# Two layers on one core: the norm of image 0 gets its own place in the order, and places and shares are settled anew

## The chip, the cores and the metric

The kernel runs on one core of a Trainium2 chip, in one launch. The core has TensorE (PE) for matmuls and transposes, VectorE (DVE), ScalarE (ACT) and GpSimd (POOL) for work on elements, and a sequencer (SP) that issues nearly all DMAs. The metric is the device time in microseconds (us); lower is better.

## The reference: a selective scan, then an attention block between convolutions

The input `x` has 4 images of 512 channels and 32 x 32 points (1024 tokens), all float32.

```
# layer 0, xn = LayerNorm over channels of GroupNorm(x)
xm, z = split(xn @ W_in)                    # 1024 channels each
xs = silu(causal depthwise conv of 4 taps (xm))
dt, B, C = parts of xs @ W_x;  dt = softplus(dt @ W_dt + b_dt)
h[t] = exp(dt[t]*A) * h[t-1] + (dt[t]*xs[t]) * B[t]     # 16 states per channel
y = sum over states of h*C + xs*D;  x = x + (y * silu(z)) @ W_out
# layer 1, on GroupNorm(x)
top, center = two 1x1 convolutions;  bottom = 3x3 convolution
x = x + conv3x3(v + softmax(center @ top) @ bottom),  v = GroupNorm(x)
```

Layer 1 can't begin on image 0 before the GroupNorm statistics of image 0's layer-0 output are there. They need only image 0, while layer 0 ends with image 3.

## The kernel before

**Stages and units.** Layer 0 treats the images one after the other. An image has 8 stages `n` (4 groups of 256 channels, `e`, by 2 halves of 512 tokens, `h`; `n = 2e + h`), and a stage has 16 units, one for each state `s`. A unit (`unit`, from L886) makes a decay with ACT exponentials (L904), a product with B, a scan on DVE (L957), a product with C, and a sum over states by accumulating transposes on PE into `y` (L990). Who makes the two products differs:

- **ACT unit**: ACT makes the product with B, transposed (four `sc` instructions, L917), PE turns it back (eight transposes into `u`, L943), DVE scans, POOL makes the product with C (L980).
- **POOL unit**: POOL makes the product with B (L932, from the row `bbc` that a DMA spreads over the partitions), DVE scans, POOL makes the product with C (L980).
- **DVE unit**: as the POOL unit, but the scan goes to PSUM and DVE makes the product with C (two of L973). In a first half, DVE copies two carries as well (L962), where POOL would copy them (L979).

The table `ACT_B[b][n]` holds the number of ACT units of a stage, and `DVE_C[b][n]` says how many of the rest are DVE units.

**The order.** Nothing of layer 0 is issued as written: each piece is a `step` with an engine, a guessed duration and a place `prio`. Unit `s` of stage `n` of image `b` has the place `(8b + n)*16 + s`, so that the images begin at 0, 128, 256 and 384 and the last unit has 511. `Plan.issue` (L149) walks through a clock of its own. On each engine it takes, among the steps that could start within `SLACK` of the soonest, the one with the lowest place. No step may be issued whose place is more than `AHEAD` beyond the lowest one still open (pieces marked `fill` don't count as open, but are held by it too). A step that needs another ACT table is held back by `TURN` times 1.3 us, unless its place is over `URGENT` lower than the best that needs none. On the chip each engine runs its instructions in the order so found.

**What else has places.** All of them are in `PRM`. For the next image: the norm (`m0`, spread by `nl`), projection with convolution (`c0`, `cg`), the parameters of the scan (`p0`, `pg`). For the present one: the gates (`g0`, `gg`), the step sizes (`dl`; `d1`, `d2` for image 0), the transposes of a unit against its other parts (`kt`, `ke`, `ka`). Then the output projection of the image before (`o0`, `og`), of the last image in parts as its stages end (`l3`, `l5`, `l6`; `last_proj`, L1103), and 18 pieces of a weight transform for layer 1 (`pc`; `transform`, L1224) that mostly run on POOL, in the tile `work`.

**The norm of image 0** (`first_image`, L1148) ends layer 0. POOL clears the rim of the padded tile (L281 to L284), in the memory that `work` had, so after the last transform piece. SP reads image 0 back in eight DMAs (L1166), DVE makes statistics (L1179, L1180), PE averages groups (L1187, L1203), ACT takes the root (L304, L305), DVE normalizes (L1217). With `fi=-5.11` and `fl=0` the loads have the place 517.11, the statistics up to the root 521.11 (`prio + 4`), the normalizing 522.11. The last gate (DVE, L1030 and L1033) has 514, the last output projection (PE, L444, into `po`) 512, 514, 516 and 518 for its four blocks, and so have the additions of `po` to `total` (DVE, L1134).

After that each engine goes on with layer 1 in the order written: PE with the scores (`pt`, L1411; `psc`, L1432) and the 3 x 3 convolutions (`m_b`, `m_o`, L1584).

Of the kernel before, what the change touches and what calls it, by code (L numbers as in the profile page):

```python
# [29 lines left out]

PRM = dict(
    xp=(1, 2, 1),
    d1=10.1,
    pg=(0.46, 0.4, 0.67, 0.61),
    kt=(0.33, 3.93, 5.81, 6.9),
    ke=(1.1, 4.93, 2.75, 4.55),
    ka=(-4.81, -1.6, -3.24, 3.25),
    dl=(9.79, 12.5, 12.12, 15.22),
    nl=(0.17, 1.94, 1.25),
    m0=(52.74, 50.42, 48.4),  # L40
    c0=(68.39, 60.05, 64.33),
    cg=(4.46, 6.19, 6.58),
    p0=(117.51, 108.54, 112.88),
    g0=(1.18, -46.47, -50.81, -55.84),
    gg=(7.81, 8.86, 8.96, 7.61),
    o0=(17.38, 16.29, 17.48),
    og=(5.73, 4.85, 7.27),
    pc=(-196.09, -39.49, -79.97, -11.49, -76.67, -112.89, -101.52, 31.36, 14.53, 57.53, 92.72, 155.74, 200.22, 264.5, 322.22, 362.01, 463.04, 499.85),
    h0=-6.05,
    hg=2.38,  # L50
    p1=3.61,
    d2=-7.19,
    fl=0,
    fi=-5.11,
    l3=69.43,
    l5=101.89,
    l6=114.08,
    il=0,
)


ACT_B = (
# [4 lines left out]
)  # L67
DVE_C = (
# [4 lines left out]
)  # L73


# [22 lines left out]
class Plan:  # L98
# [4 lines left out]
    LAG = {"PE": 0.17, "DVE": 0.095, "ACT": 0.1, "POOL": 0.06, "SP": 0.0}  # L103
    HOP = {"PE": 0.16, "DVE": 0.045, "ACT": 0.06, "POOL": 0.08, "SP": 0.05}
    BEGIN = {"PE": 5.0, "DVE": 1.5, "ACT": 9.0, "POOL": 7.0, "SP": 1.5}
    FREE, LOAD, SLACK, AHEAD = 0.06, 1.3, 0.11, 15.44
    TURN, URGENT = 1.47, 1.72

    def __init__(self, slots, in_order, exp_set):
        self.slots, self.steps, self.exp_set = dict(slots), [], exp_set  # L110
# [5 lines left out]
    def step(self, eng, us, fn, reads=(), writes=(), prio=0.0, table=None, kb=0, fill=False, holds=()):  # L116
        s = Step(eng, us, fn, prio, table, kb, fill)
        for b in holds:
            if b.first:
                s.deps.add(b.first)  # L120
            else:
                b.first = s
        for b in (*reads, *writes, *holds):
            if b in s.bufs:
                continue
            s.bufs.append(b)
            if b.ring and not b.left:
                s.takes.append(b)
                if b.ring in self.queues and not b.free:
                    self.queues[b.ring].append(b)  # L130
            b.left += 1
        for b in reads:
            if b.writer:
                s.deps.add(b.writer)
        for b in writes:
            s.deps.update(b.readers)
            if b.writer:
                s.deps.add(b.writer)
        for b in reads:
            b.readers.append(s)  # L140
        for b in writes:
            b.writer, b.readers = s, []
        s.deps.discard(s)
        for d in s.deps:
            d.users.append(s)
        s.unmet = len(s.deps)
        self.steps.append(s)
# [69 lines left out]
def mamba_then_pab_kernel(  # L217
# [60 lines left out]
    def padded(b, pool, tag):  # L278

        xg = pool.tile([P, NCC, HH + 2, WW + 2], F32, tag=tag, name=f"xg_{b}")  # L280
        nc.gpsimd.memset(xg[:, :, 0, :], 0.0)  # L281
        nc.gpsimd.memset(xg[:, :, HH + 1, :], 0.0)
        nc.gpsimd.memset(xg[:, :, 1 : HH + 1, 0], 0.0)
        nc.gpsimd.memset(xg[:, :, 1 : HH + 1, WW + 1], 0.0)  # L284
        return xg
# [16 lines left out]
    def rsqrt(out, var):  # L302

        nc.scalar.activation(out, var, AF.Ln, bias=eps)  # L304
        nc.scalar.activation(out, out, AF.Exp, scale=-0.5)  # L305

    def deviation(p, mv, mean, dev):


        nc.vector.tensor_copy(mean, p[:, :NCC])  # L310
        nc.vector.tensor_sub(dev, mv[:, :, 0], p[:, :NCC])
        nc.vector.tensor_sub(p[:, NCC : 2 * NCC], mv[:, :, 0], p[:, :NCC])
        nc.vector.tensor_mul(p[:, 2 * NCC : 3 * NCC], dev, p[:, NCC : 2 * NCC])
        nc.vector.tensor_add(dev, p[:, 2 * NCC : 3 * NCC], mv[:, :, 1])
# [8 lines left out]
    with ExitStack() as l0:  # L323
# [76 lines left out]
        step = plan.step  # L400
# [3 lines left out]
        def buf(ring, shape, name, free=False):  # L404
            if ring is None:
                return Buf(None, lambda: shape)
            if ring in cells:
                y, x = shape[1:3]
                return Buf(
                    ring,  # L410
                    lambda: cells[ring].pop(0).rearrange("p (y x o) -> p y x o", y=y, x=x),
                    done=lambda t: cells[ring].append(t.rearrange("p y x o -> p (y x o)")),
                )
            pool = {"xt": xtp, "mm": mmp, "u": up, "y0": yp, "y1": yp}.get(ring, sp)
            return Buf(
                ring,
                lambda: pool.tile(shape, F32, tag=ring, name=name, bufs=plan.slots[ring]),
                free=free,
            )
# [728 lines left out]
        def first_image(prio):  # L1148

            spl = {}  # L1150
            stat = buf(None, None, "")
            chunks = [buf(None, None, "") for c in range(NCC)]

            def inner(c):
                return image[0][:, c, 1 : HH + 1, 1 : WW + 1]

            def make():
                image[0] = padded(0, cpool, "image")

            step("POOL", 1.2, make, [], [pieces, *chunks], prio - PRM["fl"])  # L1160
            for c in range(NCC):
                for h in range(NH):
                    n = HH // NH
                    step(
                        "SP", 0.4,
                        lambda c=c, h=h, n=n: nc.sync.dma_start(  # L1166
                            inner(c)[:, h * n : (h + 1) * n, :],
                            x1[0][h][c * P : (c + 1) * P, :].rearrange("p (h w) -> p h w", w=WW),
                        ),
                        [x1s[0][h]], [chunks[c]], prio - PRM["fl"], kb=768,  # L1170
                    )

                def stats(c=c):
                    if c == 0:
                        spl["mv"] = spool.tile([P, NCC, 2], F32, tag="mv", name="mv_image")
                    bs = spool.tile([P, NH, 6], F32, tag="bs", name=f"bs_image_{c}")
                    n = HH // NH
                    for h in range(NH):
                        nc.vector.bn_stats(bs[:, h, :], inner(c)[:, h * n : (h + 1) * n, :])  # L1179
                    nc.vector.bn_aggr(spl["mv"][:, c, :], bs)  # L1180

                step("DVE", 1.45, stats, [chunks[c]], [stat], prio + 4)
            prio += 4
            pm = buf("mm", [P, T], "pm_image")
            step(
                "PE", 0.3,
                lambda: nc.tensor.matmul(  # L1187
                    pm()[:, :NCC], gm_sb, spl["mv"][:, :, 0], start=True, stop=True
                ),
                [stat], [pm], prio,  # L1190
            )

            def mid():
                spl["mean"], spl["dev"] = (
                    spool.tile([P, NCC], F32, tag=n, name=f"{n}_image") for n in ("gmean", "gdev")
                )
                deviation(pm(), spl["mv"], spl["mean"], spl["dev"])

            step("DVE", 0.75, mid, [], [pm, stat], prio)
            pv = buf("mm", [P, T], "pv_image")  # L1200
            step(
                "PE", 0.3,
                lambda: nc.tensor.matmul(  # L1203
                    pv()[:, :NCC], gm_sb, spl["dev"], start=True, stop=True
                ),
                [stat], [pv], prio,
            )

            def root():
                spl["rstd"] = spool.tile([P, NCC], F32, tag="grstd", name="grstd_image")  # L1210
                rsqrt(spl["rstd"], pv()[:, :NCC])

            step("ACT", 1.7, root, [pv], [stat], prio, "exp")
            for c in range(NCC):
                step(
                    "DVE", 0.76,
                    lambda c=c: nc.vector.tensor_scalar(  # L1217
                        inner(c), inner(c), spl["mean"][:, c : c + 1],
                        spl["rstd"][:, c : c + 1], ALU.subtract, ALU.mult,
                    ),  # L1220
                    [stat], [chunks[c]], prio + 1,
                )
# [628 lines left out]
```

## Time and profile before

| | us |
|---|---|
| median of 3 runs | 2886.27 (2882.78 to 2889.2) |
| the profiled execution | 2896.7 |
| its span, first to last instruction | 2894.9 |
| start of the last copy out of `y`, which ends image 0, 1, 2, 3 | 585.9, 1026.2, 1490.3, 1860.1 |
| first matmul of layer 1 on PE (`pt`) | 1875.8 |

In the views below, each stretch lists the busy time of each engine with the number of its instructions, then the granted clock of PE (1.00 is full) and the DMA share. A group line gives its busy time, the mean duration in nanoseconds, and the idle time just before its instructions with what ended it. A timeline line gives start, duration, engine, line, operation and tiles.

### The profile page before, as it was taken

How to read it: one execution, taken by the hardware profiler on the slowest of the kernel's cores; microseconds unless marked ns; L12 is line 12 of the kernel's file. 1: busy time of each engine (PE TensorE's matmuls, PEld its weight loads, DVE VectorE, ACT ScalarE, POOL GpSimd, SP SyncE). 2: the span in 40 equal slices, each digit the busy share in tenths (PEclk: the TensorE clock that was granted, in tenths of full speed). 3: DMA queues.
4: the chain of work that ended last, by engine and by line, in shares of the span. 5: the costliest groups of instructions: out<-in, count | busy, mean ns of one | idle time of the engine just before them, and what ended most of it. 6: DMA issues, size and time to landing. Idle time of an engine off the chain costs nothing.

```text
span 2894.9 us, 36258 instructions
## 1 busy us (share of the span) xinstructions
PE 2720.9 (94%) x11752; PEld 1628.6 (56%) x11752; DVE 2288.4 (79%) x2730; ACT 1837.1 (63%) x3250; POOL 2039.3 (70%) x1243
## 2 busy tenths in 40 slices
PE   6898799999999999989989999899999999999999
PEld 2466566666666666666667766544444444444445
DVE  4579999989999889989899999867776755346264
ACT  4789999999899999899999999530300003030000
POOL 6999999899998999999999999733241341214222
PEclk9999999999999999999999999899999999999999
DMA  6766655567655577645565664757789886536586
GB/s 182 209 178 190 190 166 176 159 216 243 197 163 167 161 230 229 200 144 179 160 203 178 210 196 147 180 215 259 257 277 304 315 322 240 188 123 240 189 318 241
DMA packets 406548, 603.68 MB, mean 209 GB/s; under 512 B 47224, under 2 KB 246136, under 8 KB 382040
## 3 DMA queue, kind: packets, MB, share of 16 engines
q1 hardware_dynamic: 398744, 587.11, 63.6%
q10 hardware_dynamic: 7616, 14.26, 1.3%
q8 instruction: 94, 1.54, 0.2%
q14 instruction: 94, 0.77, 0.1%
HBM read 504.27 MB, written 96.99 MB: 208 GB/s over the span
## 4 chain that ended last, share of the span: by engine, by line
PE 44%; ACT 19%; DVE 15%; POOL 9%; issue 6%; DMA 5%; SPq 0%; POOLq 0%; DVEq 0%; ACTq 0%
PE m_o L1584 10%; PE m_b L1584 8%; DVE da L957 5%; ACT sc L917 4%; PE y L990 4%; PE pat L1643 4%; ACT da L904 4%; PE u L943 3%; POOL da L980 3%; PE pxm L444 3%; PE po L444 3%; ACT u L904 3%; PE pz L444 2%; DVE u L957 2%; PE pp L800 1%
## 5 line engine op out<-in xcount | busy, mean ns | idle before, releaser
L980 POOL TENSOR_TENSOR da<-da,cbc 128x1024 f32<-128x1024 f32 x314 | 741.6, 2368 | 33.3 <-DVE da L957 8.3
L917 ACT ACTIVATE sc<-dtxt,bt_sb 128x256 f32<-128x256 f32 x1256 | 550.7, 499 | 17.1 <-PE u L943 16.4
L932 POOL TENSOR_TENSOR dbx<-dtx,bbc 128x1024 f32<-128x1024 f32 x198 | 467.1, 2369 | 20.2 <-PE y L990 7.8
L904 ACT ACTIVATE da<-dt,a_sb 128x512 f32<-128x512 f32 x628 | 433.7, 714 | 15.4 <-PE y L990 10.6
L957 DVE TENSOR_TENSOR_SCAN da<-da,u 128x512 f32<-128x512 f32 x328 | 383.1, 1203 | 40.5 <-PE u L943 23.3
L943 PE MATMUL u<-ident,sc 128*128 128x128 f32 x2512 | 363.1, 279 | 33.4 <-DVE da L957 19.6
L943 PEld LDWEIGHTS u<-ident,sc 128*128 128x128 f32 x2512 | 291.6, 142 | 161.6 <-issue 47.2
L957 DVE TENSOR_TENSOR_SCAN da<-da,carry_sb,u 128x512 f32<-128x512 f32 x300 | 367.2, 1260 | 13.7 <-PE u L943 10.3
L990 PE MATMUL y<-ident,da 128*128 128x128 f32 x2512 | 339.5, 277 | 27.7 <-POOL da L980 27.0
L1584 PE MATMUL m_b<-uw_b,v_b 128*128 128x512 f32 x768 | 335.2, 596 | 6.7 <-DMA uw_b<-u_b 4.4
L990 PEld LDWEIGHTS y<-ident,da 128*128 128x128 f32 x2512 | 290.3, 142 | 90.2 <-POOL da L980 49.0
L1584 PE MATMUL m_o<-uw_o,v_o 128*128 128x512 f32 x736 | 321.9, 596 | 4.2 <-DMA uw_o<-u_o 4.1
L904 ACT ACTIVATE u<-dt,a_sb 128x512 f32<-128x512 f32 x396 | 262.5, 681 | 10.7 <-DVE da L957 5.8
L444 PE MATMUL pxm<-xt,winc 128*128 128x345 f32 (+3 forms) x704 | 242.7, 488 | 18.6 <-DVE xs L706 4.7
L1584 PEld LDWEIGHTS m_b<-uw_b,v_b 128*128 128x128 f32 x768 | 145.5, 191 | 192.9 <-issue 178.6
L444 PE MATMUL pz<-xt,winc 128*128 128x512 f32 x512 | 240.3, 600 | 2.1 <-ACT dtxt L881 1.0
L1584 PEld LDWEIGHTS m_o<-uw_o,v_o 128*128 128x128 f32 x736 | 139.0, 191 | 180.2 <-issue 173.2
L990 PE MATMUL y<-ident,dbx 128*128 128x128 f32 x1584 | 219.8, 276 | 12.2 <-DVE dbx L973 7.1
L980 POOL TENSOR_TENSOR dbx<-dbx,cbc 128x1024 f32<-128x1024 f32 x91 | 215.2, 2365 | 13.8 <-DVE dbx L957 7.0
L1643 PE MATMUL pat<-y_b,st 128*128 128x512 f32 x512 | 221.6, 593 | 1.7 <-DVE rz L1654 1.6
L990 PEld LDWEIGHTS y<-ident,dbx 128*128 128x128 f32 x1584 | 182.6, 142 | 48.4 <-issue 22.1
L444 PE MATMUL po<-gt,wpr 128*128 128x512 f32 x384 | 182.4, 594 | 4.3 <-DVE u L957 2.3
(231 smaller groups left out, 4113.2 us busy)
## 6 DMA issues: line engine op xcount, KB each, us to landing
cbc<-bcd SPq DMA_DIRECT2D x512, 256.0 KB, 3.6
uw_b<-u_b SPq DMA_DIRECT2D x96, 1024.0 KB, 4.8
uw_o<-u_o SPq DMA_DIRECT2D x92, 1024.0 KB, 4.8
bbc<-bcd SPq DMA_DIRECT2D x198, 256.0 KB, 4.1
u_b<-work SPq DMA_DIRECT2D x192, 128.0 KB, 2.7
winc<-in_w_in_dram SPq DMA_DIRECT2D x72, 256.0 KB, 3.6
szd<-sz SPq DMA_DIRECT2D x32, 512.0 KB, 3.7
szl<-szd SPq DMA_DIRECT2D x32, 512.0 KB, 5.0
```

What stands on the lines that cost most here:

```text
L444: lambda k=k, lhs=lhs, rhs=rhs: nc.tensor.matmul(p()[:, at : at + cols], lhs(), rhs(), start=(k == 0), stop=(k == n - 1)),
L800: lambda d=d, hs=hs, pp=pp: nc.tensor.matmul(pp()[p0 : p0 + NP, :], wx_sb[:, d, :], xs[b, d]()[:, hs], start=(d == 0), stop=(d == NDC - 1),),
L904: nc.scalar.activation(t, dt()[:, j], AF.Exp, scale=a_sb[:, at : at + 1])
L917: nc.scalar.activation(sc()[:, k], dtxt()[:, k], AF.Copy, scale=bt[:, at, s : s + 1])
L932: lambda: nc.gpsimd.tensor_mul(hc(), dtx(), b_bc().to_broadcast([P, 2, T])),
L943: nc.tensor.transpose(u()[:, k * P : (k + 1) * P], sc()[:, k, j, :], ident)
L957: nc.vector.tensor_tensor_scan(ht, *((hc()[:, j], u()) if on_act else (u(), hc()[:, j])), carry_sb[:, j, s : s + 1] if h else 0.0, ALU.mul ...
L980: nc.gpsimd.tensor_mul(hc(), hc(), c_bc().to_broadcast([P, 2, T]))
L990: nc.tensor.matmul(y[j]()[:, k, :], hc()[:, j, k * P : (k + 1) * P], ident, start=(s == 0 and k == 0), stop=(s == NS - 1 and k == NK - 1), ...
L1584: nc.tensor.matmul(m[q], v[:, q, k, c, :], w[:, c, :], start=(c == 0), stop=(c == NCC - 1 and not extra),)
L1643: nc.tensor.matmul(pt, st[m][:, 2 * P * j + h : 2 * P * (j + 1) : 2], xb[m // 2][:, m % 2, :], start=(m == 0), stop=(m == NMC - 1),)
```

## The change

One parameter is new, `f4`: the statistics of image 0's norm have the place `fi`-based `prio + f4` in place of `prio + 4`, and all that follows them in the norm moves with them. Their guessed duration goes from 1.45 to 1.4. With the new `fi`, `fl` and `f4` the loads stand at 517.36, the statistics up to the root at 512.29, the normalizing at 513.29. Most other entries of `PRM` change too, seven entries of the two tables of shares, and `AHEAD`, `TURN` and `URGENT`. No instruction of a kind that was not there is added. Lines from `f4` on stand one line lower.

```diff
-    d1=10.1,
-    pg=(0.46, 0.4, 0.67, 0.61),
-    kt=(0.33, 3.93, 5.81, 6.9),
-    ke=(1.1, 4.93, 2.75, 4.55),
-    ka=(-4.81, -1.6, -3.24, 3.25),
-    dl=(9.79, 12.5, 12.12, 15.22),
-    nl=(0.17, 1.94, 1.25),
-    m0=(52.74, 50.42, 48.4),
-    c0=(68.39, 60.05, 64.33),
-    cg=(4.46, 6.19, 6.58),
-    p0=(117.51, 108.54, 112.88),
-    g0=(1.18, -46.47, -50.81, -55.84),
-    gg=(7.81, 8.86, 8.96, 7.61),
+    d1=6.86,
+    pg=(0.58, 0.48, 0.67, 0.62),
+    kt=(0.48, 3.9, 6.11, 5.12),
+    ke=(0.94, 4.77, 3.54, 3.15),
+    ka=(-4.68, -1.72, -2.8, 1.39),
+    dl=(8.98, 12.29, 12.22, 16.1),
+    nl=(0.45, 1.8, 0.27),
+    m0=(51.62, 55.84, 49.53),
+    c0=(68.45, 60.12, 58.81),
+    cg=(4.45, 6.01, 6.94),
+    p0=(114.15, 108.47, 112.45),
+    g0=(0.99, -46.47, -50.77, -56.39),
+    gg=(7.87, 9.01, 9, 8.85),
...
-    pc=(-196.09, -39.49, -79.97, -11.49, -76.67, -112.89, -101.52, 31.36, 14.53, 57.53, 92.72, 155.74, 200.22, 264.5, 322.22, 362.01, 463.04, 499.85),
+    pc=(-133.37, -10.07, -212.91, -41.13, -178.93, -177.05, -56.54, 31.33, 13.69, 56.22, 87.13, 151.52, 201.63, 264.84, 321.08, 366.48, 465.52, 501.27),
...
-    p1=3.61,
-    d2=-7.19,
-    fl=0,
-    fi=-5.11,
-    l3=69.43,
-    l5=101.89,
-    l6=114.08,
+    p1=7.51,
+    d2=-6.07,
+    fl=-17.79,
+    fi=12.43,
+    l3=82.11,
+    l5=103.8,
+    l6=116.99,
+    f4=12.72,
...
 ACT_B = (
     (12, 8, 10, 7, 9, 7, 8, 8),
-    (10, 12, 12, 8, 10, 8, 8, 8),
-    (12, 8, 13, 8, 9, 7, 10, 8),
-    (8, 13, 11, 13, 11, 13, 11, 14),
+    (10, 12, 12, 8, 10, 7, 8, 8),
+    (12, 8, 13, 8, 9, 7, 10, 7),
+    (8, 13, 11, 12, 11, 13, 11, 14),
 )
 DVE_C = (
     (2, 6, 6, 4, 1, 3, 5, 5),
-    (3, 4, 4, 4, 1, 4, 1, 4),
-    (4, 4, 3, 1, 1, 4, 1, 7),
-    (5, 2, 3, 1, 5, 3, 4, 2),
+    (5, 4, 4, 4, 1, 5, 2, 5),
+    (4, 4, 3, 1, 1, 3, 1, 8),
+    (5, 2, 3, 2, 5, 3, 3, 2),
 )
...
-    FREE, LOAD, SLACK, AHEAD = 0.06, 1.3, 0.11, 15.44
-    TURN, URGENT = 1.47, 1.72
+    FREE, LOAD, SLACK, AHEAD = 0.06, 1.3, 0.11, 15.93
+    TURN, URGENT = 2.57, 1.71
...
-                step("DVE", 1.45, stats, [chunks[c]], [stat], prio + 4)
-            prio += 4
+                step("DVE", 1.4, stats, [chunks[c]], [stat], prio + PRM["f4"])
+            prio += PRM["f4"]
```

The other changed entries (`o0`, `og`, `h0`, `hg`) move by less than half a unit.

More of the change, by code (lines that the diff above doesn't have):

```diff
@@ L32 @@
     xp=(1, 2, 1),
-    d1=10.1,
-    pg=(0.46, 0.4, 0.67, 0.61),
-    kt=(0.33, 3.93, 5.81, 6.9),
-    ke=(1.1, 4.93, 2.75, 4.55),
-    ka=(-4.81, -1.6, -3.24, 3.25),
-    dl=(9.79, 12.5, 12.12, 15.22),
-    nl=(0.17, 1.94, 1.25),
-    m0=(52.74, 50.42, 48.4),
-    c0=(68.39, 60.05, 64.33),
-    cg=(4.46, 6.19, 6.58),
-    p0=(117.51, 108.54, 112.88),
-    g0=(1.18, -46.47, -50.81, -55.84),
-    gg=(7.81, 8.86, 8.96, 7.61),
-    o0=(17.38, 16.29, 17.48),
-    og=(5.73, 4.85, 7.27),
-    pc=(-196.09, -39.49, -79.97, -11.49, -76.67, -112.89, -101.52, 31.36, 14.53, 57.53, 92.72, 155.74, 200.22, 264.5, 322.22, 362.01, 463.04, 499.85),
-    h0=-6.05,
-    hg=2.38,
-    p1=3.61,
-    d2=-7.19,
-    fl=0,
-    fi=-5.11,
-    l3=69.43,
-    l5=101.89,
-    l6=114.08,
+    d1=6.86,
[11 more added lines that the diff above has]
+    gg=(7.87, 9.01, 9, 8.85),
+    o0=(17.18, 16.67, 17.05),
+    og=(5.76, 4.78, 7.35),
+    pc=(-133.37, -10.07, -212.91, -41.13, -178.93, -177.05, -56.54, 31.33, 13.69, 56.22, 87.13, 151.52, 201.63, 264.84, 321.08, 366.48, 465.52, 501.27),
+    h0=-6.08,
+    hg=2.37,
+    p1=7.51,
[6 more added lines that the diff above has]
+    f4=12.72,
     il=0,
```

## The prediction, made before the changed kernel ran

> **What bounds the kernel now.** I read three views: the page's group rows for prices, the stretches of the trace for the load of each part, and the timeline around the end of layer 0.
>
> The stretches are the ramp, the scans of images 0 to 3 (cut where `y` is last copied out), the handover, and layer 1:
>
> ```profile
> core 0: us, PE busy (x) PEld busy (x) DVE busy (x) ACT busy (x) POOL busy (x), PEclk, DMA share, GB/s
> 0.00:186.00 186.00, 150.05 (x521) 76.29 (x522) 102.60 (x165) 121.72 (x201) 150.42 (x143) 0.98 0.67 185
> 186.00:586.00 400.00, 359.29 (x1955) 249.44 (x1954) 380.88 (x452) 384.51 (x650) 380.16 (x226) 0.97 0.61 179
> 586.00:1026.00 440.00, 420.50 (x2314) 290.64 (x2315) 408.94 (x473) 410.41 (x725) 412.65 (x248) 0.99 0.62 191
> 1026.00:1490.00 464.00, 440.05 (x2359) 299.86 (x2357) 419.52 (x482) 433.32 (x756) 432.43 (x268) 0.98 0.61 188
> 1490.00:1860.00 370.00, 340.04 (x2145) 253.79 (x2146) 359.01 (x390) 350.70 (x681) 358.94 (x220) 0.98 0.63 188
> 1860.00:1901.00 41.00, 36.11 (x78) 16.08 (x78) 30.32 (x37) 15.80 (x31) 20.62 (x13) 0.82 0.38 111
> 1901.00:2895.00 994.00, 974.81 (x2388) 442.48 (x2386) 587.14 (x736) 120.62 (x212) 284.10 (x129) 0.99 0.72 254
> ```
>
> In the scans four engines are busy 90 to 97% at once, so no single one sets the pace: an order that avoids waits gains, and load moved from one engine to another hardly does. Layer 1 is PE's (974.81 of 994), so whatever starts it earlier is kept to the end. The handover is bad: PE at 0.82 of its clock, everybody else idle half the time.
>
> ```profile
> 1845.62 13.89 SPq L1166 DMA_DIRECT2D xg<-x  x8
> ...
> 1863.21 0.69 DVE L1033 TENSOR_TENSOR xs<-pyb,szl 128x512 f32<-128x512 f32 x1
> ...
> 1871.15 1.28 DVE L1179 BATCH_NORM_STATS2 bs_image<-xg 128x6 f32<-128x512 f32 x2
> ...
> 1872.73 0.39 PE L1187 MATMUL pm_image<-mv_image,gm_sb 128*128 128x4 f32 x2 [0.50 <-DVE mv_image L1180]
> ...
> 1875.80 9.87 PE L1411 MATMUL pt<-xg,wt_sb 128*128 128x512 f32 x16 [1.51 <-DVE xg L1217]
> ```
>
> SP's loads of image 0 end their issue at 1859.5 and land a median of 5.7 later. The statistics only start behind the last gate (1863.8), the fourth group even behind the third addition to `total`, because its place is 521. So PE, done with `po` at 1872.2, waits for the norm.
>
> ```profile
> 1855.00:1861.00 6.00, 4.01 (x22) 3.42 (x23) 0.54 (x1) 1.17 (x2) 3.02 (x2) 0.70 1.58 142
> 1861.00:1864.00 3.00, 2.23 (x6) 0.99 (x6) 2.90 (x5) 0.00 (x0) 0.00 (x0) 0.50 0.82 69
> ...
> 1872.00:1876.00 4.00, 1.19 (x6) 0.80 (x6) 2.88 (x10) 0.47 (x2) 3.46 (x7) 0.81 0.81 229
> 1876.00:1880.00 4.00, 4.00 (x5) 1.60 (x6) 2.62 (x3) 1.29 (x2) 1.87 (x2) 0.50 1.00 410
> ```
>
> DVE is nearly idle from 1855 to 1861, when the statistics could run. PE is idle from 1872.2 to 1875.8 and then runs at half clock.
>
> **Part 1, the norm of image 0: -6.** The statistics go from 521.11 to 512.29, below the gate's 514; the normalizing goes to 513.29. The loads' place hardly changes (517.11 to 517.36), but they may come earlier: `AHEAD` grows by 0.49, and the lowest open place (that of a unit's accumulation, `s - ka`) grows by 3.25 - 1.39 = 1.86. Together that is 2.1 units after the loads' own 0.25; a stage of image 3 took 43.9 to 51.2, so a unit is about 3 us and the loads can go some 6 us earlier. That puts the last landing near 1859 instead of 1865. The limit is the last transform piece (499.85 to 501.27, some 4 us later; it ended at 1826.0 against loads at 1845.6, so there is room). Eight statistics with four aggregations are about 6.0 us (four of 1.28 + 0.21): they fill the idle 5.5. What follows (five DVE operations of 0.7 in all, two small PE products, 0.5 on ACT, 3.8 of normalizing) then lies beside the 9.6 of `po`. PE goes from `po` to `pt` at 1872.2. Saved: the idle 3.6, less 0.8 of `pm` and `pv` that stay, so 2.8. The 16 `pt` took 9.87 and at the full-clock spacing of 0.43 take 6.9: 3.0 more. Sum 5.8, call it 6. From below: the loads stay late, and only the two additions ahead of the fourth statistics go, 2 x 0.7 = 1.4. On the other side the early loads take SP's queue: they issue in 13.9 us (1.7 each against 0.3 for another), and the last two `cbc` rows issue just ahead (1842.3). Put behind two loads, each row comes 3.4 late and POOL, which multiplies with it, too: +3, less the 1.4. Ends: -6 and +2; I take -6, as SP's rows have the lower place and the idle time lies ready.
>
> A rule of the Trainium skill bears on the half clock (TensorE: Matmul & The Clock Gate, Part 1: The HAM clock gate): PE falls to half rate after an idle window of about 3.4 us and needs about as long a busy one to leave it. The trace agrees: 3.6 idle, then 0.50. By the rule a wait cut only to 3.5 us would save nothing of the 3.0; the sum above doesn't rest on it.
>
> **Part 2, the shares: -2.** Counted from the tables: ACT units 314 to 311, POOL-made B products 198 to 201, DVE units 107 to 112, other POOL-made C products 91 to 89.
>
> ```profile
> L980 POOL TENSOR_TENSOR da<-da,cbc 128x1024 f32<-128x1024 f32 x314 | 741.6, 2368 | 33.3 <-DVE da L957 8.3
> L917 ACT ACTIVATE sc<-dtxt,bt_sb 128x256 f32<-128x256 f32 x1256 | 550.7, 499 | 17.1 <-PE u L943 16.4
> L943 PE MATMUL u<-ident,sc 128*128 128x128 f32 x2512 | 363.1, 279 | 33.4 <-DVE da L957 19.6
> L973 DVE TENSOR_TENSOR dbx<-u,cbc 128x512 f32<-128x512 f32 x214 | 140.5, 672 | 0.1
> ```
>
> ACT: 3 x 4 x 0.499 = -6.0. PE: 24 x (363.1/2512 = 0.145) = -3.5. POOL: two products fewer, -4.7. DVE: five units of 2 x 0.672, and two carry copies of 0.158 for the two (net) in first halves: +7.3. Three more `bbc` loads cost their SP issue, 0.3 each, in a queue that is mostly waiting. By stage (image, stage):
>
> ```profile
> 867.00:922.00 55.00, 53.96 (x288) 37.24 (x287) 53.27 (x63) 54.44 (x90) 46.71 (x24) 1.00 0.52 157
> 922.00:977.00 55.00, 53.15 (x290) 36.11 (x290) 50.91 (x60) 52.67 (x90) 53.96 (x37) 1.00 0.53 159
> ...
> 1432.00:1490.00 58.00, 57.44 (x295) 34.36 (x294) 55.93 (x60) 53.83 (x89) 49.43 (x25) 1.00 0.61 170
> ```
>
> In (1,5), the first, ACT and PE are full and get 2.0 and 1.2 less, for 1.34 more on DVE, which has 1.7 free: -1. In (1,6) POOL is the fullest and loses a product, but PE is close behind: -0.8. In (2,7) PE is full and gets 1.2 less: -1. In (1,0) DVE has 6.9 free for its 3.3. In (2,5), (3,3), (3,6) the fullest engine trades about even; (3,6) is tight for POOL, which gets 2.4 with 1.8 free: +0.8. Sum -2. The ends: all of DVE's 7.3 comes on top, or the largest relief (ACT's 6.0) is kept in full. I take -2, from the rows of the stages themselves.
>
> **Part 3, table switches: -1.** `TURN` goes from 1.47 to 2.57: a switch waits until ACT would idle 3.3 instead of 1.9 in the planner's clock. The four load groups count 75 + 31 + 29 + 19 = 154, at 1.28 each. Most come because they are overdue, which doesn't change. I guess four fewer: 5 us of ACT, a fourth of it on the path: -1. Ends -6 (a tenth fewer, 15 x 1.28 = 19 us, a third kept) and +3 (a softplus that comes 2 us later, twice).
>
> By the Trainium skill (ScalarE: Activation LUTs, What ACT_TABLE_LOAD costs) a switch costs 1.28 for the load and 1.38 of drain, which would double the 5 us. The trace shows no drain: an exponential ended at 1257.55, the load began at 1257.56, the next operation at 1258.86.
>
> **Part 4, places of the next image: -3.** Of these, image 3's entry stands out: its norm is drawn together (`nl` 1.25 to 0.27) and its convolution begins 5.5 units earlier (`c0` 64.33 to 58.81). In stretches of 5 us, PE idles 7.9 us between 1240 and 1275, behind that norm and ahead of the products of the convolution, while later (2,7) it is full. Filling the hole gains up to 7.9; I take 3, as part of it is waits of single units on ACT and DVE. Ends -7.9 and +9.2 (one episode of the second rival). The rest (`kt`, `ke`, `ka`, `dl`, gates, `pc`) reorders without removing: zero, with 5 to either side. The early `pc` keep their sum: six pieces stay ahead of place -20, one at about -10.
>
> **Sum.** -6 - 2 - 1 - 3 = -12: the profiled execution would go from 2896.7 to 2884.7. It lies 10.4 above the median of the runs shown, so the forecast for the median is 2886.3 - 12 = 2874.3, say 2874.
>
> **Rivals.**
> - *The handover stays as it is* (the loads still land behind the last gate, or another wait replaces this one), and the reordering evens out: only 1.4 and the shares' 2 are left, 2883. For it: the last load lands near 1865 now, and only the planner's own clock decides whether SP gets to it sooner. Against it: 5.5 idle us on DVE and 19.6 us between the last piece and the loads. Chance 0.18; it counts as no change, since about 0.2%, 5.8 us, is what a measurement here can tell apart.
> - *The norm of a next image starves PE* and ends slower. Place: around 1200 to 1225 in image 2. There PE was idle 4.1 us in five stretches of 5 and its clock read 1.00, 0.89, 0.50, 0.59 and 1.00, worth 0.5 + 2.5 + 2.1 = 5.1 more: 9.2 an episode. Drawn together, image 3's norm puts more of its chain ahead of the units, so that such an episode comes again. It decides when PE idles about 4 of 10 us, as from 1200 to 1210. Two more turn the sum round: 2874.3 + 18.4 = 2893, three give 2902. For it: images 1 and 2 each show such a dip already (0.50 at 785 too). Against it: the convolution comes sooner behind the norm. Chance 0.20.
> - *The order pays more*: one of the two dips goes (-9.2) and the hole closes whole (-4.9 more): 2860. Chance 0.14.
>
> **Chances and range.** The forecast has the remaining 0.48, so faster 0.48 + 0.14 = 0.62, same 0.18, slower 0.20. The range of 2856 to 2894 takes in each part's ends and two episodes; I leave out a tenth on either side.
>
> **What would show it.** Right: L1179 (one line lower after) ahead of or between the last gates, `pt` within 1 us of the last `po`, clock near 1 in `pt`; fewer than 154 table loads; PE over 4 of 5 us behind image 3's norm; image 1 no longer than 440, image 2 shorter than 464. Wrong: L1166 issuing ahead of `cbc` rows with POOL waiting for them, new stretches at 0.50 in the scans, or image 1 longer with DVE full, which would make part 2 the failing step.

## The result, and the profile after

The changed kernel takes 2877.32 us (median of 10 runs, 2872.7 to 2884.3); before takes 2890.19 on the same chip (10 runs, 2882.78 to 2896.85). The ratio is **0.9958, interval 0.9946 to 0.997**: 12 us less by the ratio, 13 by the medians, where 12 were forecast. The profiled executions took 2880.61 (changed) and 2896.7 (before). They lie 3.3 and 6.5 us above their medians, so the profiles differ by 16 us.

First the same seven stretches of the changed kernel (us; busy time of PE, PEld, DVE, ACT and POOL with counts; PE's clock; DMA share; GB/s), cut at the same events as before:

```profile
0.00:181.00 181.00, 149.34 (x520) 75.78 (x521) 102.52 (x165) 122.07 (x201) 150.65 (x143) 0.99 0.69 191
181.00:584.00 403.00, 364.04 (x1952) 252.67 (x1953) 380.39 (x453) 382.38 (x644) 379.45 (x224) 0.96 0.60 178
584.00:1018.00 434.00, 417.40 (x2306) 288.46 (x2306) 416.31 (x488) 412.39 (x728) 403.12 (x243) 0.99 0.62 194
1018.00:1470.00 452.00, 431.63 (x2339) 297.00 (x2338) 414.00 (x478) 426.25 (x745) 433.95 (x266) 0.98 0.63 194
1470.00:1845.00 375.00, 345.39 (x2151) 255.13 (x2150) 362.59 (x392) 352.94 (x682) 362.26 (x224) 0.98 0.63 186
1845.00:1884.00 39.00, 33.02 (x78) 14.40 (x77) 29.25 (x37) 15.55 (x30) 20.62 (x13) 0.92 0.42 120
1884.00:2879.00 995.00, 974.95 (x2390) 442.74 (x2388) 586.72 (x736) 120.88 (x213) 283.20 (x129) 0.99 0.72 253
```

Cut to a tenth, before and after (image 0 with its ramp; the handover runs from the start of the last copy of `y` to the first `m_b`):

| | image 0 | image 1 | image 2 | image 3 | handover | layer 1 |
|---|---|---|---|---|---|---|
| before | 585.9 | 440.3 | 464.1 | 369.8 | 40.7 | 994.1 |
| after | 584.2 | 433.9 | 451.8 | 375.4 | 39.1 | 994.4 |
| difference | -1.7 | -6.4 | -12.3 | +5.6 | -1.6 | +0.3 |

So by these two profiles 14.8 of 16.2 come from the scans, where I had looked for 6, and 1.6 from the handover, where I had also looked for 6. A run further down (the norm's place alone) issues all scans in the order of before. Its profile has 584.5, 436.9, 463.5 and 370.1 for the images and 39.2 for the handover (whose order differs a little there): against it the scans gain 9.8. The scans' share is thus some 10 to 15 us.

Over images 1 to 3 the engines do about the same work (from 6.2 us less on PE to 5.4 more on DVE) in 13 us less. Part of the work of image 2 moved into image 3, so their differences belong together. In image 1 DVE is idle for 17.7 us where it was 31.1, ACT for 21.6 (29.6).

Now the end of layer 0, the timeline that the prediction showed of before:

```profile
1830.97 14.63 SPq L1167 DMA_DIRECT2D xg<-x  x8
...
1846.20 0.75 DVE L1031 SCALAR_TENSOR_TENSOR pyb<-xs,dp_sb,pyb 128x512 f32<-128x512 f32 x1 [5.73 <-PE pyb L1024]
...
1855.12 1.28 DVE L1180 BATCH_NORM_STATS2 bs_image<-xg 128x6 f32<-128x512 f32 x2
...
1856.70 0.38 PE L1188 MATMUL pm_image<-mv_image,gm_sb 128*128 128x4 f32 x2 [0.50 <-DVE mv_image L1181]
...
1859.77 1.13 PE L1412 MATMUL pt<-xg,wt_sb 128*128 128x512 f32 x2 [1.51 <-DVE xg L1218]
...
1861.21 7.99 PE L1412 MATMUL pt<-xg,wt_sb 128*128 128x512 f32 x14 [0.32 <-DVE xg L1218]
```

The loads are issued 15 us earlier, but only because all of layer 0 ends 15 us earlier: the first stands 14.3 us ahead of the last copy of `y`, where it stood 14.5 ahead. The first statistics start at 1848.98, still behind the last gate, though DVE is idle for 5.73 us ahead of the first gate (the bracket in the second line), and the fourth still stands behind the third addition to `total`. `po` ends at 1856.20 and `pt` starts at 1859.77, the same 3.6 us as before. After that gap PE reads a clock of 0.66 from 1860 to 1864. The chain that the change is named after still hands over late.

### The profile page after: what moved, and what is told of

It is laid out like the page before. It is cut to its first block, busy times and chain, and to the rows that moved or that the text cites. A ratio compares the mean times of both kernels' runs of the same rounds, so it can differ in the third digit from the quotient of the medians.

```text
span 2878.7 us, 36221 instructions
## 1 busy us (share of the span) xinstructions
PE 2715.8 (94%) x11728; PEld 1626.2 (56%) x11728; DVE 2291.8 (80%) x2744; ACT 1832.5 (64%) x3238; POOL 2033.3 (71%) x1239
## 4 chain that ended last, share of the span: by engine, by line
PE 42%; DVE 21%; ACT 14%; POOL 9%; issue 6%; DMA 6%; SPq 1%; DVEq 0%; POOLq 0%; ACTq 0%
PE m_o L1585 11%; PE m_b L1585 8%; DVE da L958 6%; PE y L991 4%; POOL da L981 4%; PE pat L1644 4%; ACT sc L918 3%; PE u L944 3%; PE po L445 3%; ACT da L905 2%; DVE u L958 2%; DVE dbx L958 2%; PE pxm L445 2%; PE pz L445 2%; ACT u L905 2%
## 5 line engine op out<-in xcount | busy, mean ns | idle before, releaser
L933 POOL TENSOR_TENSOR dbx<-dtx,bbc 128x1024 f32<-128x1024 f32 x201 | 474.3, 2369 | 17.9 <-PE y L991 8.8
L944 PE MATMUL u<-ident,sc 128*128 128x128 f32 x2488 | 361.0, 279 | 29.7 <-DVE da L958 14.5
L958 DVE TENSOR_TENSOR_SCAN da<-da,carry_sb,u 128x512 f32<-128x512 f32 x294 | 360.1, 1260 | 11.4 <-PE u L944 5.7
L445 PE MATMUL pxm<-xt,winc 128*128 128x345 f32 (+3 forms) x704 | 244.7, 489 | 11.4 <-DVE xs L707 3.8
L991 PEld LDWEIGHTS y<-ident,dbx 128*128 128x128 f32 x1608 | 188.4, 143 | 41.8 <-issue 22.5
```

What stands on the lines that cost most here:

```text
L445: lambda k=k, lhs=lhs, rhs=rhs: nc.tensor.matmul(p()[:, at : at + cols], lhs(), rhs(), start=(k == 0), stop=(k == n - 1)),
L933: lambda: nc.gpsimd.tensor_mul(hc(), dtx(), b_bc().to_broadcast([P, 2, T])),
L944: nc.tensor.transpose(u()[:, k * P : (k + 1) * P], sc()[:, k, j, :], ident)
L958: nc.vector.tensor_tensor_scan(ht, *((hc()[:, j], u()) if on_act else (u(), hc()[:, j])), carry_sb[:, j, s : s + 1] if h else 0.0, ALU.mul ...
L991: nc.tensor.matmul(y[j]()[:, k, :], hc()[:, j, k * P : (k + 1) * P], ident, start=(s == 0 and k == 0), stop=(s == NS - 1 and k == NK - 1), ...
```

## The experiments

Two theories stand against each other. **S**: the parts are worth something each, and the worths add up. **J**: the planner's whole order decides; each part alone, or the whole without one part, is another order with waits of its own, and one part's worth doesn't exist apart from the others. J has a gauge that comes from the kernel: the end of layer 0 in the planner's own clock, 1835.9 for before and 1827.7 for after. It is a guess made of guessed durations, so the runs test it too. All ratios are to before, run on the same chip.

**The tables of shares alone, in the kernel before.**

```diff
-ACT_B, DVE_C = tables of before
+ACT_B, DVE_C = tables of after
```


> Before, with the two tables of shares of the change and nothing else of it. In the planner's own clock layer 0 then ends at 1855.1 instead of 1835.9 (after the whole change: 1827.7). Theory J (the gain belongs to the order as a whole, found by settling all numbers together; a part put into the old order loses): slower than before by 8 to 20 us, ratio 1.003 to 1.007. Theory S (the parts of the prediction add up, each keeps its worth alone): 2 us faster, ratio 0.998 to 1.000.

Measured: 2915.7 us, ratio 1.0103 (1.0086 to 1.012). Image 1 takes 452.4 where it took 440.3:

```profile
584.00:1036.00 452.00, 423.47 (x2304) 291.16 (x2302) 416.97 (x488) 409.39 (x721) 402.17 (x242) 0.98 0.59 187
```

DVE has 8 us more to do than in the row of before, POOL 10 less and ACT as much as it had, in 12 us more: no engine got full, all wait longer (ACT is idle 42.6 us, was 29.6). A forecast from loads can't see that.

**`AHEAD`, `TURN` and `URGENT` alone, and all places but those of image 0's norm alone, in the kernel before.**

```diff
-FREE, LOAD, SLACK, AHEAD = 0.06, 1.3, 0.11, 15.44
-TURN, URGENT = 1.47, 1.72
+FREE, LOAD, SLACK, AHEAD = 0.06, 1.3, 0.11, 15.93
+TURN, URGENT = 2.57, 1.71
```


> Before, with AHEAD, TURN and URGENT of the change and nothing else of it. The planner's own clock ends at 1847.6 instead of 1835.9, with 154 table switches instead of 156. Theory J: slower by 4 to 12 us, ratio 1.0015 to 1.004. Theory S: 1 us faster for fewer switches, ratio 0.999 to 1.000.

```diff
-PRM = places of before
+PRM = places of after, but fl, fi and the statistics' place as before
```


> Before, with all places of PRM of the change except fl, fi and f4, and with the old shares, AHEAD, TURN and URGENT. The planner's own clock ends at 1842.5 instead of 1835.9. Theory J: slower by 2 to 8 us, ratio 1.0005 to 1.003. Theory S: 3 us faster from the places, ratio 0.998 to 1.000; if the measured gain of 12 sits in the places alone, 0.996.

Measured: 1.005 (1.0034 to 1.0065) and 1.0031 (1.0016 to 1.0047). Each of the three parts alone is a loss, that of the tables and that of the constants larger than J had expected (1.007 and 1.004 at most).

**The changed kernel with the old tables.**

```diff
-ACT_B, DVE_C = tables of after
+ACT_B, DVE_C = tables of before
```


> The changed kernel with the two tables of shares of before. The planner's own clock ends at 1843.5 (before 1835.9, after 1827.7). Theory J: slower than before by 2 to 9 us, ratio 1.0005 to 1.003, so the change loses its whole gain when 14 of its numbers are taken out. Theory S: the change's gain less 2 us, ratio 0.9955 to 0.9975.

Measured: 1.0029 (1.0016 to 1.0041). Against the changed kernel's 0.9958 the tables are worth 0.7% there; alone they cost 1.0%. The sign of a part depends on its company, which S can't hold. (The tables differ in eleven entries, three of `ACT_B` and eight of `DVE_C`, and not in seven or 14 as it says above.)

**The place of image 0's norm alone**, the part that names the change.

```diff
-fl=0, fi=-5.11, statistics at prio + 4
+fl=-17.79, fi=12.43, statistics at prio + f4, f4=12.72
```


> Before, with fl, fi and f4 of the change and nothing else of it: the norm of image 0 has the changed place, all scans are issued as before. On DVE the first statistics now stand between the two last gates, the others among the additions to total as before. In the changed kernel itself the old fl, fi and f4 give the very same order on every engine. Part 1 of the prediction: 6 us faster, ratio 0.998. Rival (the place decides nothing, since in the planner's clock the loads of image 0 land only as the last gates end): no change, ratio 0.999 to 1.001.

Measured: 1.0007 (0.9998 to 1.0015), no difference. In its profile the first statistics stand between the last two gates, and `pt` waits 1.8 us behind `po` where it waited 3.6; that is too little to show in the time. The converse needs no run: with these three old values put back into the changed kernel, the planner finds the same order on all five engines, instruction by instruction. The reason is in the planner: it costs each of the eight loads as 768 KB, and both halves of a chunk write one buffer, so that the second waits for the first. In its clock the data land only as the gates end (in the kernel before, the first chunk at 1819.2 and the last at 1826.9; the last gate is done at 1821.1), and a lower place doesn't start statistics whose data aren't there.

The four single changes sum to +1.03 + 0.50 + 0.31 + 0.07 = +1.9%, or 55 us. Together they give -0.4%.

**One place, moved by 0.02.** If the order is what counts, a change that means nothing must do something.

```diff
-    gg=(7.87, 9.01, 9, 8.85),
+    gg=(7.87, 8.99, 9, 8.85),
```


> The changed kernel with one number moved: the spacing of image 1's gates, gg, 8.99 instead of 9.01. No instruction is added or taken out, two table switches fewer (154). The planner's own clock ends its last output projection at 1830.5 instead of 1819.7. Theory J, sharpened by the first runs (1 us of the planner's clock is 1.1 to 1.5 us on the chip, whatever was changed): 12 to 16 us slower than the changed kernel, so level with before, ratio 0.9995 to 1.0015. Theory S: two switches fewer are worth 0.5 us, the move of a place by 0.02 nothing: ratio 0.995 to 0.997.

Measured: 1.0006 (0.9997 to 1.0015). 0.02 of a unit in the gates of image 1 takes the whole gain. Image 1 goes from 433.9 to 446.4; 10.3 of that is its stage 2, of 50.8 us after and 61.1 here. The timeline of that stage, first PE, then ACT:

```profile
708.82 1.98 PE L445 MATMUL pd<-proj,wdt_sb 128*128 128x512 f32 x4 [1.43 <-ACT dtxt L882]
...
732.73 13.98 PE L445 MATMUL po<-gt,wpr 128*128 128x512 f32 x32
...
731.99 1.23 ACT L850 ACTIVATE dt<-pd,bdt_sb 128x512 f32<-128x512 f32 x2
...
747.18 0.91 ACT L918 ACTIVATE sc<-dtxt,bt_sb 128x256 f32<-128x256 f32 x2 [5.67 <-PE u L944]
```

and its stretches:

```profile
732.00:740.00 8.00, 8.00 (x25) 3.99 (x25) 5.67 (x7) 7.95 (x13) 7.75 (x4) 1.00 0.48 130
740.00:748.00 8.00, 8.00 (x30) 4.25 (x29) 4.28 (x5) 2.31 (x6) 3.81 (x3) 1.00 0.87 229
```

PE runs 16 products of the output projection (two passes each in the trace) as one block. Each group of eight needs one of two PSUM buffers, `mm`. In the planner's clock their operand `gt` lands at 691.4, in the changed kernel at 685.6. In between, two products `pd` for the step sizes of stage 4 take both buffers, and ACT reads these only at 731.99. By then the place of the output products is below that of the units, and all go first. The transposes of `sc` queue behind them on PE: ACT waits 5.67 until they have read `sc`, DVE and POOL wait for their input. PE is full throughout, so that a look at PE alone would praise it. In this stage of the changed kernel the output products start at 705.23 and come at most 10 passes at a time, ahead of those `pd` (733.45):

```profile
724.00:732.00 8.00, 8.00 (x40) 5.03 (x40) 8.00 (x9) 6.28 (x14) 7.92 (x5) 1.00 0.52 170
```

The run with `AHEAD`, `TURN` and `URGENT` alone has this block too: stage 2 of image 1 is 62.9 there and 53.3 in before.

**The block spread out.** Is the block the loss, or its sign?

```diff
+                if e == "PE" and row >= 2 and 700 < clock["PE"] < 735:
+                    rest = [f for f in found if f[4].us != 0.875 and f[0] < clock["PE"] + 1.0]
+                    found = rest or found
...
+            if s.eng == "PE":
+                row = row + 1 if s.us == 0.875 else 0
```
(a product of 512 columns, as in the output projection, is a step of 0.875 us; the base is the run with the gates' 8.99)

> The kernel with the gates' place of image 1 moved by 0.02, and in it the planner may not issue more than two products of the output projection in a row while its clock of TensorE stands between 700 and 735 us, if another step of TensorE could start within 1 us. The 16 products of one piece that stood in one block in stage (1,2) (PE 14.0 us, ScalarE idle 5.7 us behind it) then come two at a time between the scores. The end of layer 0 by the planner's clock stays at 1838.5 us and the table switches at 154, as without the cut. Theory that the block itself is the lost time: ScalarE's wait of 5.7 us goes, stage (1,2) shrinks from 61.1 us by 6 to 10, and the ratio to before falls to 0.997 to 0.9985. Theory that the order as a whole decides (the planner's end is the same): the block is only spread out, the stage or the one behind it gives the time back, and the ratio stays level with the kernel without the cut, 0.9995 to 1.0015.

Measured: 1.0005 (0.9997 to 1.0014), level with the block's 1.0006. The wait went, as both theories held:

```profile
732.00:740.00 8.00, 8.00 (x34) 4.45 (x33) 8.00 (x9) 8.00 (x17) 7.87 (x4) 1.00 0.37 129
740.00:748.00 8.00, 8.00 (x32) 4.38 (x31) 6.49 (x7) 7.45 (x11) 8.00 (x5) 1.00 0.77 182
748.00:756.00 8.00, 7.50 (x44) 5.21 (x43) 7.71 (x10) 4.29 (x9) 4.06 (x3) 1.00 1.01 316
```

Between 732 and 748 ACT, DVE and POOL work through, and from 748 to 756 ACT is busy for 4.29 of 8. Stage 2 went from 61.1 to 51.9 and stage 3 from 45.7 to 55.4: the sum stays. The products have to be done before the next image's norm gets its buffer `xt`, and they still start only when `mm` comes free: at 732.73 with the block, at 732.56 spread out. They end at 775.13 and 775.33, in the changed kernel at 763.74, and each time the load of `xt` is issued 0.03 us later. So the most visible wait was not the loss. The late end of the products fits the loss: 11.4 us, of the 12.5 that image 1 lost.

**A transform piece one unit earlier**, in the changed kernel.

```diff
-    pc=(..., 56.22, ...),
+    pc=(..., 55.22, ...),
```


> The changed kernel with one piece of the weight transform (the tenth) one unit, some 3 us, earlier: 55.22 instead of 56.22. The same instructions, but 150 table switches instead of 156, so 7.7 us less of ACT. The planner's own clock ends its last output projection 13 later. Part 3 of the prediction (a fourth of the spared switches counts): 2 us faster than the changed kernel, ratio 0.994 to 0.996. Theory J: 14 to 19 us slower than the changed kernel, ratio 1.0005 to 1.0025.

Measured: 1.0009 (0.9998 to 1.002). The gain is gone again, and this order has 151 table loads in the trace, six fewer than before and after.

**Image 3's entry put back**, in the changed kernel: the part I had singled out.

```diff
-    nl, m0, c0, cg, p0 of image 3: 0.27, 49.53, 58.81, 6.94, 112.45
+    nl, m0, c0, cg, p0 of image 3: 1.25, 48.4, 64.33, 6.58, 112.88
```


> The changed kernel with image 3's entry of before: nl, m0, c0, cg and p0 of that image alone (lag of the norm 1.25 instead of 0.27, convolution 5.5 units later). 152 table switches instead of 156; the planner's own clock ends its last output projection 7.9 later than in the changed kernel. Part 4 of the prediction: 3 us slower than the changed kernel, all of it in image 2, ratio 0.996 to 0.9975. Theory J (1.1 to 1.5 us for 1 us of the planner's clock): 9 to 12 us slower than the changed kernel, ratio 0.9985 to 1.001.

Measured: 0.9988 (0.9979 to 0.9997). The entry is worth 0.3% inside the changed order, some 9 us. By stage (4 to 7 of image 2, where image 3's norm and convolution run):

| | stage 4 | 5 | 6 | 7 | sum |
|---|---|---|---|---|---|
| before | 74.2 | 62.0 | 53.3 | 58.5 | 248.0 |
| entry put back | 71.6 | 52.0 | 60.3 | 58.4 | 242.3 |
| after | 64.4 | 59.5 | 65.8 | 47.4 | 237.1 |

Stage 3, in which that norm begins, takes 58.1, 59.7 and 56.2.

In the stretch behind the norm, first the changed kernel, then the one with the entry put back:

```profile
1250.00:1270.00 20.00, 18.02 (x91) 11.78 (x90) 19.65 (x28) 19.87 (x29) 17.87 (x14) 1.00 0.48 151
```

```profile
1250.00:1270.00 20.00, 15.24 (x91) 11.48 (x92) 19.37 (x26) 18.80 (x30) 19.06 (x14) 1.00 0.55 146
```

PE is idle 4.8 of 20 us without the earlier convolution and 2.0 with it.

**A norm that really is early.** If the handover's chain was rightly seen and only not moved, moving it must pay. The eight loads now go, at a place of 400, into five tiles of the scan's rings that are free by then (so neither `work` nor the gates hold them), at their true 256 KB and each half with a buffer of its own. Statistics stand from 430 on, the normalizing at 511; it reads those tiles and writes the padded one.

```diff
-                            inner(c)[:, h * n : (h + 1) * n, :],
-                            x1[0][h][c * P : (c + 1) * P, :].rearrange("p (h w) -> p h w", w=WW),
+                            v(), x1[0][h][c * P : (c + 1) * P, :]
...
-                        [x1s[0][h]], [chunks[c]], prio - PRM["fl"], kb=768,
+                        [x1s[0][h]], [landed[h]], PRM["f_load"], kb=256, holds=[bs_[h][0]],
...
-                step("DVE", 1.4, stats, [chunks[c]], [stat], prio + PRM["f4"])
+                step("DVE", 1.45, stats, landed, [stat], PRM["f_stat"] + PRM["f_gap"] * c, ...)
```


> The changed kernel with the norm of image 0 rebuilt: its loads go to buffers that are free in image 3 (two of xs, sz, the two of win) instead of the padded tile, have the place 400, the statistics 430 to 454, the root 462, the clearing of the rim 500, the normalizing into the padded tile 511, ahead of the last gate; no other number is settled anew. The planner's own clock ends its last output projection 5.3 later than in the changed kernel. Handover (last copy out of y to the first m_b) 33 us instead of 39, as pt follows the last po at once and at full clock; scans 6 to 8 us longer by Theory J: level with the changed kernel, ratio 0.995 to 0.9975. If the handover is held by something else behind the norm (the rim of the next image, f_b on POOL, the first v_b on DVE), it keeps its 39 and the kernel is 6 us slower than the changed one, ratio 0.9975 to 0.9995.

Measured: 2875.45 us, 0.995 (0.9934 to 0.9965). The total isn't told apart from the changed kernel's 0.9958 (0.9946 to 0.997). In the profile the handover falls from 39.1 to 30.5; images 2 and 3 give 4.0 of that back. The end of layer 0 in its stretches:

```profile
1843.00:1848.00 5.00, 3.25 (x20) 2.25 (x20) 5.00 (x6) 0.55 (x2) 3.70 (x2) 1.00 0.00 0
1848.00:1853.00 5.00, 5.00 (x18) 2.45 (x17) 4.42 (x8) 0.52 (x2) 0.00 (x0) 1.00 0.00 0
1853.00:1859.00 6.00, 6.00 (x15) 2.66 (x14) 2.06 (x3) 0.00 (x0) 0.00 (x0) 1.00 0.23 87
```

The loads were issued at 1484 to 1497 and the statistics ran from 1600 to 1675, in gaps of the scans. DVE normalizes from 1843.92, ahead of the gates, and PE takes `pt` among the last `po` with no gap over 0.6 us, at full clock.

**The early norm with the order settled anew for it**: two dozen places that the kernel still reads, six shares and `URGENT` (the expectation counts 27 and seven), chosen by the planner's clock alone.

> early0 with 27 places, seven shares and URGENT settled anew in the planner's own clock for the rebuilt norm: its last output projection ends at 1817.7 instead of 1825.0. Theory J: 8 to 11 us faster than early0, ratio to before 0.991 to 0.9925, so clearly faster than the changed kernel too. Theory S: what is moved here removes no work (ACT units 313 instead of 311, DVE units 110 instead of 112), so it is level with early0, ratio 0.994 to 0.996.

Measured: **2865.98 us, ratio 0.9926 (0.9911 to 0.994)**, the best of all: 21 us below before and below the changed kernel, whose interval begins at 0.9946. The intervals of this run and the one before it overlap a little, so the worth of the new settling alone isn't clear of noise. Its stretches are 579.8, 434.5, 455.3, 373.0, 32.7 and 992.8.

**The gauge.** The end of layer 0 in the planner's clock, beside what the chip gave:

| kernel | planner's end | ratio |
|---|---|---|
| after | 1827.7 | 0.9958 |
| image 3's entry put back | 1835.6 | 0.9988 |
| before | 1835.9 | 1 |
| norm's place alone | 1836.4 | 1.0007 |
| gates' place, 0.02; block spread out | 1838.5, 1838.5 | 1.0006, 1.0005 |
| transform piece | 1840.8 | 1.0009 |
| places alone | 1842.5 | 1.0031 |
| old tables | 1843.5 | 1.0029 |
| three constants alone | 1847.6 | 1.005 |
| tables alone | 1855.1 | 1.0103 |

A straight line through these eleven has a slope of 1.5 us on the chip for each of the clock's, and none lies more than 3.2 us off it. So the planner's end tells the time of an order to some 3 us, whichever part was changed. The two kernels with the early norm (1830.6 and 1823.3) gain their handover behind that point and are left out.

## Why the prediction was right, and which of its steps were not

The total came out (-12 forecast, ratio 0.9958, 2877.3 against 2874), but not by its working. The handover gave 4 us less than forecast and the scans 4 to 9 more, and the two misses cancelled: that the time was hit is luck.

- **Bound.** That four engines are full in turn and only waits can go held: images 1 to 3 lost 13 us, while no engine's busy time moved by more than 6.2.
- **Part 1, the norm of image 0 (-6): wrong.** The step that failed is "the statistics fill the idle 5.5": a place only ranks steps that are ready, and the planner's clock has the data landing as the gates end. Measured: -1.6 in the profiles; as a single change a wait of 1.8 instead of 3.6 and no difference in the time; the changed order the same without it. That the loads go 6 us earlier was wrong too: against the end of layer 0 they stayed where they were (14.5 and 14.3 us ahead). The price of the chain itself was fair: moved in earnest, it took 8.6 off the handover, though the total of that run doesn't show it clear of noise.
- **The clock behind the gap** was seen rightly: as the 3.6 us of waiting stayed, so did a clock of 0.66; without the gap it read 1.00. By the Trainium skill (TensorE: Matmul & The Clock Gate, Part 1: The HAM clock gate) PE goes to half rate after an idle window of about 3.4 us. The drop behind the gap fits that, though the gap holds two small products (`pm_image`, `pv_image`, 0.4 each). A drop came without such a gap as well: in the changed kernel the clock reads 0.56 from 1840 to 1846, where PE had had no idle time over 1.6 us since 1829.
- **Part 2, the shares (-2): wrong as a term.** Loads were counted rightly (1244 `sc`, 224 products of DVE), though the list of stages left out (1,7), where DVE gets a unit more. But the worth of a move isn't in the loads: +1.0% in one order, -0.7% in the other.
- **Part 3, four fewer table loads (-1): wrong.** There are 157 in either trace (the four groups counted hold 154). And six fewer, in the run with the moved transform piece, came with a longer time.
- **Part 4, places (-3): right in direction and place, too small.** The entry of image 3 alone carries some 9 us inside the changed order. The hole between 1240 and 1275 explains a part only: shifted ten us down with the image's earlier start, PE is idle 5.4 there instead of 7.9. "The rest reorders without removing: zero" was the mis-sized term: stages 4 to 7 of image 2 lost 10.9 and image 1 lost 6.4 (3.1 against the second profile of before's order).
- **Rivals.** The first one's mechanism happened (the handover stayed), without its time, because the order paid elsewhere as in the third. The second didn't decide: near 1200 the clock still dips (0.83 from 1190 to 1210), where before dips from 1210 to 1230 (0.77): one dip for another.
- **Signs.** Image 1 under 440 and image 2 under 464 came true, and PE over 4 of 5 us behind image 3's norm nearly (one stretch has 3.75). `pt` within 1 us of `po`, statistics ahead of the gates and fewer table loads didn't. The handover's signs told at once that the time came from somewhere else.

**What stays open**: most of the chain from 0.02 of a place to that block of products. Its start is a rank that turns: the fifth gate projection of image 1 goes from 117.57 to 117.49, past the scan's parameters at 117.51, and in the planner's clock the orders part there, at 513.4 in image 0. Its end is the later `gt` and the taken `mm`. What lies between, and which single choices make the other orders longer, was not followed.

## What to carry to other kernels

Where a list scheduler writes the order, don't price its parameters one by one: a part has no worth outside the order, and the largest visible wait may be a sign and not the loss (here of buffers that a later stage had taken early). Price the order as a whole (here by the scheduler's own end time, which the chip followed), and look at a step's readiness in that clock before moving its place. A transfer that is costed too dear, or that shares a buffer with another, keeps late what a place should bring early; here the planner's clock shows it, and the run with the early norm changed place, cost and buffers together.

## What was unexpected of the hardware

The same order can run into another clock. With the norm's place alone, image 1's order is that of before, yet it took 436.9 us and not 440.3. The matmuls of image 2's norm, in before and in that run:

```profile
788.01 9.32 PE L444 MATMUL pmu<-xt,mw 128*128 128x512 f32 x16
```

```profile
785.94 7.11 PE L445 MATMUL pmu<-xt,mw 128*128 128x512 f32 x16
```

PE's clock reads 0.51 from 782 to 790 and 0.85 to 798 in before, and 0.79 from 780 to 788 and then 1.00 in the other. One profile is good to some 3 us an image, no better. The Trainium skill (TensorE: Matmul & The Clock Gate, Part 1: The HAM clock gate) states that the gate's window runs freely, so that the same kernel meets it at different phases; these two rows fit that.
